# Softmax denominators of a decoder layer: partition sums by VectorE block transposes in 37 group halves, gated sums ahead in 4 instead of 19

## The chip, the cores and the metric

The kernel runs on one core of one Trainium2 chip. A core has TensorE (PE, matmuls into PSUM), VectorE (DVE), ScalarE (ACT), GpSimd (POOL) and SyncE (SP, which here only issues DMAs). The metric is the device time of one execution in microseconds, as the median of the runs. Everything is computed in float32.

## The reference

One decoder layer on x of shape (4, 1024, 512): a gated self-attention, a cross-attention to a context of shape (4, 1024, 384), and a small feed-forward network, each behind a layer norm and added to x. What matters here are the two attentions, 16 heads of 32 each:

```python
# phase 0, self-attention
attn = softmax(q @ k.T / sqrt(32))                       # over the keys
attn = attn * aperture[q] * expression[k]                # two gates per head
attn = attn / (attn.sum(keys) + 1e-8)
out  = attn @ v
# phase 1, cross-attention
out  = softmax(q @ k.T / sqrt(32)) @ v
```

With e = exp(scores), phase 0 needs two sums over the keys for every head and query: the plain one, S = sum e, and the gated one, G = sum e * expression. The output is (e * expression) @ v, divided by G + 1e-8 * S / aperture. Phase 1 needs S alone.

## The kernel before

The work is cut into eight units u: phase 0 for the batches 0 to 3 (u = 0 to 3), then phase 1 for them (u = 4 to 7). A unit has two halves hf of 512 queries each, a half has four groups g of four heads. A triple (u, hf, g) is a group half; there are 64. Each of them runs over eight key tiles kt of 128 keys, so there are 512 steps.

A step (`step`, with `scores` and `times`) does this. TensorE computes the scores of four heads (L641) with the keys on the partitions and 512 queries along the free dimension, into two PSUM tiles of two heads; ScalarE takes the exponential of each (L647) into a tile e of shape 128 x 2 x 512. The pool of e has six buffers, that is three steps. One step later TensorE multiplies e with the values (L707, into the PSUM tile av). Between steps stands other work of TensorE, spread by `run` and `beside`: the projections of the next unit, the output projection of the last (L107) and the feed-forward network. Every engine has its instructions in the order in which the program issues them; nothing is reordered at run time.

The sums over keys are sums over partitions and over key tiles. They are made in several ways:

- es[0] (heads 0 and 1): VectorE adds the eight e tiles, elementwise (L669, L671), into a 128 x 2 x 512 tile. In phase 0 it also adds e times the gate into eg (L678 on ScalarE for the first key tile, L679). In phase 1 es[1] (heads 2 and 3) is added in the same way.
- Phase 0, heads 2 and 3: TensorE sums over the partitions. For every two key tiles one round of four matmuls (L717, in `times`) with two columns, ones and the gate, accumulates into the PSUM tile sm.
- `gated` names 19 group halves in which VectorE adds the first 4 or 6 key tiles of heads 2 and 3 ahead, plain into exa (L685, L687) and gated into exb (L691 on ScalarE, L692), so that one round of L717 over exa and exb stands for the rounds of those key tiles.

When a group half ends, `normalize` (called one step late, in the step of the next group's key tile 0) copies av and sm out of PSUM (L733, L735) and leaves `add_up` for the next step, behind that step's scores. `add_up` sums es and eg (or both es) over the partitions by one more round of four matmuls with a column of ones (L746), lets ScalarE copy the result (L747), and sends it through DRAM (L752 to L762) so that the 4 x 512 sums come back as 128 x 16, in the tile c. `divide`, two steps later, computes the reciprocal on VectorE (L770 to L785) and sends it through DRAM again (L786, L790) to 128 x 512; `multiply` (L797), two steps after that, scales the unnormalised output in q. es0 and es1 have one buffer each; eg shares its buffer with es1. In the last unit most groups are summed in a mixed way (`shared`, `added_up`), and the last group half closes in a way of its own (`settle`).

Two functions put things off: `after(n, f)` runs f n steps later, at the head of that step, before its scores, or behind them where it says `behind`.

```python
c, s1, s2 = cs_[i % 2], sum1_d[i % 4], sum2_d[i % 4]
after(apart(g), lambda: divide(g, i, c))
```

All DMAs named here are issued by SP, in one queue, where an issue that waits holds back those behind it.

Of the kernel before, what the change touches and what calls it, by code (L numbers as in the profile page):

```python
# [10 lines left out]
F32 = mybir.dt.float32  # L11
U32 = mybir.dt.uint32
AF = mybir.ActivationFunctionType
ALU = mybir.AluOpType
AX = mybir.AxisListType

P = 128
B, T, D = 4, 1024, 512
H, DH = 16, 32
NPR = H // 2  # L20
HG = 4
# [4 lines left out]
HALF = 512  # L26
M, INNER = 64, 16
# [12 lines left out]
NB = 32  # L40
# [29 lines left out]
def moderate_path(tc: tile.TileContext, a: dict, out: bass.AP, flag: bass.AP):  # L70
    nc = tc.nc
    x = a["x"]
    with ExitStack() as st:
        enter = st.enter_context
        const = enter(tc.tile_pool(name="mconst", bufs=1))
        dram = enter(tc.tile_pool(name="mdram", bufs=1, space=bass.MemoryType.DRAM))
# [4 lines left out]
        p1 = enter(tc.tile_pool(name="mp1", bufs=1))  # L81
        p2 = enter(tc.tile_pool(name="mp2", bufs=2))
# [35 lines left out]
        iap_d = [[dram.tile([H, HALF], F32, tag=f"iap_{b}_{i}", name="iap_d") for i in range(2)] for b in range(B)]  # L118
        sum1_d = [dram.tile([HG, HALF], F32, tag=f"sum1_{i}", name="sum1_d") for i in range(4)]
        sum2_d = [dram.tile([2, HG, HALF], F32, tag=f"sum2_{i}", name="sum2_d") for i in range(4)]  # L120
        rec_d = [dram.tile([HG, HALF], F32, tag=f"rec_{i}", name="rec_d") for i in range(4)]
        wout_d = dram.tile([P, NC, D], F32, name="wout_d")

# [2 lines left out]
        fixed = const.tile([P, 3], F32, name="fixed")  # L126
        ones, share, power = (fixed[:, i : i + 1] for i in range(3))
        pick = const.tile([P, 3], F32, name="pick")
        nc.gpsimd.memset(pick, 0.0)
        nc.gpsimd.memset(pick[:, 1:2], 1.0)  # L130
        for one, is_ in ((ones, 1.0), (power, -0.5), (share, 1.0 / M)):
            nc.gpsimd.memset(one, is_)

        NS = 2 * B * 2 * HG
        marks = const.tile([P, 2 * NS + B * NT], F32, name="marks")
# [56 lines left out]
        cs = p1.tile([P, 2, NC], F32, name="cs")  # L192
# [107 lines left out]
        av = pa.tile([P, HALF], F32, tag="av", name="av")  # L300
        nc.vector.memset(av, 0.0)
        sm = pa.tile([P, HALF], F32, tag="sm", name="sm")
        nc.vector.memset(sm, 0.0)


        cs_ = [const.tile([P, 2, 2, INNER], F32, name=f"cs{i}") for i in range(2)]
        for t in cs_:
            nc.gpsimd.memset(t, 0.0)

        S = {}  # L310
        crossing = []
# [62 lines left out]
        def after(steps, f, behind=False):  # L374

            soon.append((tick[0] + steps, behind, f))
# [236 lines left out]
        def attention(u, hf):  # L613

            ph, b = order[u]
            me = S[u]
            steps = []
            sums = 2 if ph == 0 else 1

            def shared(g):  # L620
                return ph == 0 or (u + 1 == len(order) and not (g == 1))

            added_up = {(0, 0): (0, 4), (0, 2): (0,), (0, HG - 1): (0, 4), (1, 0): (0,), (1, 2): (0,)} if u + 1 == len(order) else {}

            gated = {(0, 1, 0): 4, (0, 1, 1): 4, (0, 1, 2): 4, (0, 1, 3): 6, (1, 0, 0): 4, (1, 1, 0): 4, (1, 1, 1): 4, (1, 1, 2): 4, (1, 1, 3): 6, (2, 0, 0): 4, (2, 1, 0): 6, (2, 1, 1): 4, (2, 1, 2): 4, (2, 1, 3): 6, (3, 0, 0): 4, (3, 0, 3): 4, (3, 1, 0): 4, (3, 1, 1): 4, (3, 1, 3): 4}

            def apart(g):
                return 2 if u + 1 < len(order) else 3
# [100 lines left out]

            def normalize(g):  # L730
                i = (u * 2 + hf) * HG + g
                both = p1.tile([P, 2, HALF], F32, tag="both", name="both")
                nc.scalar.copy(me["q", hf][:, g, :], av)  # L733
                if shared(g):
                    nc.scalar.copy(both[:, 0, :], sm)  # L735
                    added = [me["es"][0][:, 0, :], me["es"][0][:, 1, :]]
                    if ph == 0:
                        added += [me["eg"][:, 0, :], me["eg"][:, 1, :]]
                else:
                    added = [me["es"][h // 2][:, h % 2, :] for h in range(HG)]  # L740
                after(1, lambda: add_up(g, i, both, added), behind=True)

            def add_up(g, i, both, added):

                for j, e in enumerate(added):
                    nc.tensor.matmul(sm[j * DH : j * DH + 1, :], lhsT=ones, rhs=e, start=True, stop=True)  # L746
                nc.scalar.copy(both[:, 1, :], sm)  # L747

                c, s1, s2 = cs_[i % 2], sum1_d[i % 4], sum2_d[i % 4]
                rows = both.rearrange("(j r) s q -> j r s q", r=DH)  # L750
                n = len(added)
                nc.sync.dma_start(s1[0:n], rows[0:n, 0, 1, :])  # L752
                if not shared(g):
                    nc.sync.dma_start(c[:, 0, 0, :], s1[0:n].rearrange("h (q e) -> (h q) e", e=INNER))
                else:
                    for k in range(sums):
                        nc.sync.dma_start(s2[k], rows[:, k, 0, :])
                    nc.sync.dma_start(
                        c[0:64, 0:sums, 0, :], s1[0:n].rearrange("(s h) (q e) -> (h q) s e", h=2, e=INNER)
                    )  # L760
                    for k in range(sums):
                        nc.sync.dma_start(  # L762
                            c[64:, k, :, :], s2[k].rearrange("(p h) (q e) -> (h q) p e", h=2, e=INNER)
                        )
                after(apart(g), lambda: divide(g, i, c))

            def divide(g, i, c):
                if shared(g):
                    both_ = p2.tile([P, sums, INNER], F32, tag="c2", name="both_")
                    nc.vector.tensor_tensor(both_, c[:, 0:sums, 0, :], c[:, 0:sums, 1, :], ALU.add)  # L770
                else:
                    both_ = c[:, 0:1, 0, :]
                if ph == 0:

                    den = p2.tile([P, INNER], F32, tag="den", name="den")
                    nc.vector.scalar_tensor_tensor(
                        den, both_[:, 0, :], 1e-8, me["iap", hf][:, g, :], ALU.mult, ALU.mult
                    )
                    nc.vector.tensor_tensor(den, den, both_[:, 1, :], ALU.add)
                else:  # L780
                    den = both_[:, 0, :]
                rec = p2.tile([P, INNER], F32, tag="rec", name="rec")
                nc.vector.reciprocal(rec, den)
                nc.vector.tensor_reduce(marks[:, i : i + 1], den, AX.X, ALU.add)
                nc.vector.tensor_reduce(marks[:, NS + i : NS + i + 1], rec, AX.X, ALU.add)  # L785
                nc.sync.dma_start(rec_d[i % 4].rearrange("j (q e) -> (j q) e", e=INNER), rec)  # L786

                all_ = p1.tile([P, HALF], F32, tag="recb", name="recb")
                for j in range(HG):
                    nc.sync.dma_start(  # L790
                        all_[j * DH : (j + 1) * DH, :], rec_d[i % 4][j : j + 1, :].to_broadcast([DH, HALF])
                    )
                after(apart(g) + (u + 1 == len(order) and g < 2), lambda: multiply(g, all_), behind=u + 1 < n or g < HG - 1)

            def multiply(g, all_):
                own = me["q", hf][:, g, :]
                nc.vector.tensor_tensor(own, own, all_, ALU.mult)  # L797
                me["divided", hf] = g
# [22 lines left out]
        def settle(u, hf, g):  # L821

            me = S[u]
            i = (u * 2 + hf) * HG + g
            rec = p1.tile([P, HALF], F32, tag="recb", name="recb")
            den = p1.tile([P, 2, HALF], F32, tag="both", name="den")[:, 0, :]
            few = p2.tile([P, INNER], F32, tag="rec", name="few")
            column = den.rearrange("p (b j) -> p b j", j=NB)[:, :, 0]

            def sums():  # L830
                me["by ones"](me["rest"], False, False)
                me["by ones"](me["e", NT - 1], False, True)

            def divide(part):
                cols, own = ts(part, HALF // 2), ts(part, INNER // 2)
                nc.vector.transpose(den[:, cols], sm[:, cols])
                nc.vector.reciprocal(few[:, own], column[:, own])
                nc.vector.transpose(rec[:, cols], few[:, own].unsqueeze(2).to_broadcast([P, INNER // 2, NB]))
                nc.vector.tensor_tensor(me["q", hf][:, g, cols], av[:, cols], rec[:, cols], ALU.mult)

            def look():
                nc.vector.tensor_reduce(marks[:, i : i + 1], column, AX.X, ALU.add)
                nc.vector.tensor_reduce(marks[:, NS + i : NS + i + 1], few, AX.X, ALU.add)

            return sums, divide, look
# [377 lines left out]
        p = pres[0]  # L1223
# [28 lines left out]
        sums, divide, look = settle(n - 1, 1, HG - 1)  # L1252
# [8 lines left out]
        h = [part for item in held[0]["h"] for part in item]  # L1261
# [671 lines left out]
```

## Time and profile before

| | |
|---|---|
| runs, median | 2135.34 us (2134.0 to 2136.43, three runs) |
| profiled execution | 2137.01 us, of which the span is 2135.2 us |
| granted TensorE clock | 0.998 of full speed |
| L641, scores | 7992 records, 589.3 us busy |
| L707, e times values | 4096 records, 548.2 us busy |
| L717 on e and the gates | 688 records, 89.5 us busy |
| L746, sums of es and of eg | 356 and 128 records, 65.3 and 32.8 us busy |
| L679, gated additions into eg | 448, 315.2 us busy |
| L692, gated additions into exb | 130, 91.4 us busy |
| L685 and L687, additions into exa | 19 and 46, 23.1 and 55.9 us busy |

A row of the profile names the line of the kernel, the engine, the operation, the tile that is written and those that are read, how often it ran, its busy time and the mean of one. Busy times of matmuls overlap: four matmuls on 32 columns each run side by side, so a row's sum is less than count times mean. One float32 matmul appears as two records. The span is cut into 40 slices whose digits are tenths of busy time; a timeline gives start and duration of each instruction, merged where the same follows itself, with the idle time before it and what ended it in brackets.

### The profile page before, as it was taken

What the parts mean: (1) busy time and instruction counts of PE and PEld (TensorE: products, weight loads), DVE (VectorE), ACT (ScalarE), POOL (GpSimd) and SP (SyncE); (2) the same over time, 40 slices, a digit from 0 to 9 for tenths busy, and PEclk for the clock granted to TensorE, in tenths of its full rate; (3) what the DMA queues carried; (4) which work ended last, traced back from release to release, by engine and by line L of the source; (5) the groups of instructions that cost most, each with busy time, mean ns of one, the idle gap of its engine ahead of it and who ended that gap; (6) DMA issues with size and microseconds to landing.
All of it is one profiled execution on the core that took longest, in us unless ns stands there. A gap on an engine that the chain in (4) does not pass through costs nothing.

```text
span 2135.2 us, 52477 instructions
## 1 busy us (share of the span) xinstructions
PE 2118.0 (99%) x22380; PEld 551.5 (26%) x22380; DVE 1677.9 (79%) x2468; ACT 1255.8 (59%) x1537; POOL 139.3 (7%) x184
## 2 busy tenths in 40 slices
PE   9999999999999999999999999999999999999998
PEld 5322222222222222222222222222222222222223
DVE  3477789888898888977889666887788778778887
ACT  0156555655556565565766666565655656567774
POOL 2000000040030100001000010000000000000001
PEclk9999999999999999999999999999999999999999
DMA  5422234132231212212222212231432213232231
GB/s 149 118 71 54 68 82 125 25 83 78 77 109 42 86 39 71 72 43 72 67 77 72 72 52 71 83 99 51 106 86 81 81 52 71 71 91 70 73 91 50
DMA packets 154495, 161.79 MB, mean 76 GB/s; under 512 B 47366, under 2 KB 93062, under 8 KB 153100
## 3 DMA queue, kind: packets, MB, share of 16 engines
q1 hardware_dynamic: 150188, 156.26, 25.4%
q8 instruction: 177, 2.90, 0.6%
q0 software_dynamic: 2080, 0.98, 0.3%
q10 hardware_dynamic: 1984, 1.12, 0.2%
q14 instruction: 66, 0.54, 0.1%
HBM read 115.53 MB, written 42.73 MB: 74 GB/s over the span
## 4 chain that ended last, share of the span: by engine, by line
PE 55%; DVE 1%; issue 0%; ACT 0%; DVEq 0%; ACTq 0%
PE f L107 19%; PE s L641 15%; PE av L707 14%; PE sm L746 2%; PE sm L717 2%; PE f L990 1%; PE f L641 1%; PE f L1068 0%; PE s L107 0%; DVE res L1076 0%; PE f L1024 0%; DVE es L671 0%; ACT e L647 0%; PE s L1068 0%; PE sm L697 0%
## 5 line engine op out<-in xcount | busy, mean ns | idle before, releaser
L647 ACT ACTIVATE e<-s 128x1024 f32<-128x1024 f32 x999 | 971.6, 1023 | 684.9 <-PE s L641 479.6
L671 DVE TENSOR_TENSOR es<-es,e 128x1024 f32<-128x1024 f32 x541 | 649.7, 1226 | 123.2 <-ACT e L647 121.9
L641 PE MATMUL s<-q,k 32*64 32x512 f32 x7992 | 589.3, 613 | 0.5 <-ACT e L647 0.2
L707 PE MATMUL av<-e,v 128*32 128x512 f32 x4096 | 548.2, 603 | 0.0
L107 PE MATMUL f<-xT,w 128*32 128x512 f32 x2816 | 333.7, 592 | 0.7 <-DVE xT L347 0.7
L679 DVE SCALAR_TENSOR_TENSOR eg<-e,sw,eg 128x512 f32<-128x512 f32 x448 | 315.2, 744 | 9.0 <-ACT eg L678 9.0
L669 DVE TENSOR_TENSOR es<-e 128x1024 f32<-128x1024 f32 x96 | 114.7, 1221 | 188.3 <-ACT e L647 176.6
L107 PE MATMUL f<-w,q 128*32 128x512 f32 x1984 | 238.6, 592 | 0.2
L641 PEld LDWEIGHTS s<-q,k 32*64 32x64 f32 x7992 | 129.1, 129 | 415.9 <-ACT e L647 199.5
L707 PEld LDWEIGHTS av<-e,v 128*32 128x32 f32 x4096 | 87.8, 108 | 402.9 <-issue 402.5
L107 PEld LDWEIGHTS f<-xT,w 128*32 128x32 f32 x2816 | 91.8, 110 | 211.4 <-issue 205.2
L107 PE MATMUL f<-w,xT 128*32 128x512 f32 x896 | 106.0, 592 | 0.6 <-DVE q L321 0.6
L107 PEld LDWEIGHTS f<-w,q 128*32 128x32 f32 x1984 | 64.7, 110 | 150.4 <-issue 142.2
L107 PE MATMUL f<-ctxT,w 128*32 128x512 f32 x768 | 92.3, 592 | 0.0
L107 PE MATMUL f<-w,ctxT 128*32 128x512 f32 x768 | 92.3, 592 | 0.0
L692 DVE SCALAR_TENSOR_TENSOR exb<-e,sw,exb 128x512 f32<-128x512 f32 x130 | 91.4, 743 | 0.0
L899 POOL TENSOR_TENSOR r<-res,bo_bc 128x512 f32<-128x512 f32 x32 | 40.9, 1279 | 747.0 <-DVE res L891 598.9
L717 PE MATMUL sm<-e,sw 128*2 128x512 f32 x688 | 89.5, 592 | 0.0
L327 POOL TENSOR_SCALAR rs<-fmv 128x4 f32<-128x4 f32 (+2 forms) x18 | 11.9, 659 | 833.6 <-DVE fmv L896 833.3
L746 PE MATMUL sm<-es,fixed 128*1 128x512 f32 x356 | 65.3, 591 | 0.0
L687 DVE TENSOR_TENSOR exa<-exa,e 128x1024 f32<-128x1024 f32 x46 | 55.9, 1216 | 0.0
L891 DVE TENSOR_TENSOR res<-f,res 128x512 f32<-128x512 f32 x62 | 42.4, 683 | 16.6 <-PE f L107 9.6
(293 smaller groups left out, 1354.7 us busy)
## 6 DMA issues: line engine op xcount, KB each, us to landing
recb<-rec_d SPq DMA_DIRECT2D x252, 64.0 KB
xT<-rows_d SPq DMA_DIRECT2D x60, 256.0 KB
rows_d<-r SPq DMA_DIRECT2D x60, 256.0 KB
w<-in_xattn_Wo SPq DMA_DIRECT2D x9, 1024.0 KB
w<-wout_d SPq DMA_DIRECT2D x8, 1024.0 KB
res<-in_x SPq DMA_DIRECT2D x32, 256.0 KB
x1b_d<-r SPq DMA_DIRECT2D x32, 256.0 KB
res<-x1b_d SPq DMA_DIRECT2D x32, 256.0 KB
```

The source lines that it names most:

```text
L107: nc.tensor.matmul(to[r], lhsT=lhsT[:, j, :] if len(lhsT.shape) == 3 else lhsT[:, r], rhs=rhs, **flags)
L641: nc.tensor.matmul(two[j][m : m + 64], lhsT=k[r, g, kt * P + m : kt * P + m + 64], rhs=q[r, g, :], start=True, stop=True,)
L647: nc.scalar.activation(e[:, h, :] if len(reads) == 1 else e[:, h.start, :], s, AF.Exp, scale=SCALE)
L669: nc.vector.tensor_tensor(me["es"][i], me["e", begin][i], es[i], ALU.add)
L671: nc.vector.tensor_tensor(me["es"][i], me["es"][i], es[i], ALU.add)
L679: nc.vector.scalar_tensor_tensor(eg, es[0][:, h, :], gate(kt), eg, ALU.mult, ALU.add)
L687: nc.vector.tensor_tensor(me["ep"], me["ep"], es[1], ALU.add)
L692: nc.vector.scalar_tensor_tensor(et, es[1][:, h, :], gate(kt, h), et, ALU.mult, ALU.add)
L707: nc.tensor.matmul(av[r, :], lhsT=me["v"][:, kt, HG * g + h, :], rhs=es[h // 2][:, h % 2, :], start=(kt == 0), stop=(kt == NT - 1),)
L717: nc.tensor.matmul(sm[j * DH : j * DH + sums, :], lhsT=lhsT, rhs=rhs, start=start, stop=stop)
L746: nc.tensor.matmul(sm[j * DH : j * DH + 1, :], lhsT=ones, rhs=e, start=True, stop=True)
L891: nc.vector.tensor_tensor(r, res["po"], r, ALU.add)
```

## The change

In 37 group halves (`flat`: 26 of phase 0, 11 of phase 1) a new function `fold` takes the place of `add_up`. VectorE transposes each of the four 128 x 512 sums in blocks of 32 x 32, reading the elements of a block 16 apart, and reduces the transposed blocks along the free dimension. That leaves one partial sum for each quarter of the partitions. They go to DRAM (`parts_d`) and come back side by side as four columns (`four`), and `divide` adds the four. `turn(0)` runs in `normalize`, in the step of the next group's key tile 0, `turn(1)` and the DMAs at the head of the step after; `divide` stays where it was. `gated` has four entries instead of nineteen, all with 4 key tiles. The transposes write into exa's buffer in phase 0 and into that of `both` in phase 1. The two cleared tiles `cs_` become one tile `four`, whose unwritten half is no longer read. Three memsets of constants at the start stand ahead of two others.

```diff
         sum2_d = [dram.tile([2, HG, HALF], F32, tag=f"sum2_{i}", name="sum2_d") for i in range(4)]
+        parts_d = [dram.tile([P, HG, INNER], F32, tag=f"parts_{i}", name="parts_d") for i in range(4)]
         rec_d = [dram.tile([HG, HALF], F32, tag=f"rec_{i}", name="rec_d") for i in range(4)]
...
         pick = const.tile([P, 3], F32, name="pick")
+        for one, is_ in ((ones, 1.0), (power, -0.5), (share, 1.0 / M)):
+            nc.gpsimd.memset(one, is_)
         nc.gpsimd.memset(pick, 0.0)
         nc.gpsimd.memset(pick[:, 1:2], 1.0)
-        for one, is_ in ((ones, 1.0), (power, -0.5), (share, 1.0 / M)):
-            nc.gpsimd.memset(one, is_)
 
...
 
-        cs_ = [const.tile([P, 2, 2, INNER], F32, name=f"cs{i}") for i in range(2)]
-        for t in cs_:
-            nc.gpsimd.memset(t, 0.0)
 
...
 
-            gated = {(0, 1, 0): 4, (0, 1, 1): 4, (0, 1, 2): 4, (0, 1, 3): 6, (1, 0, 0): 4, (1, 1, 0): 4, (1, 1, 1): 4, (1, 1, 2): 4, (1, 1, 3): 6, (2, 0, 0): 4, (2, 1, 0): 6, (2, 1, 1): 4, (2, 1, 2): 4, (2, 1, 3): 6, (3, 0, 0): 4, (3, 0, 3): 4, (3, 1, 0): 4, (3, 1, 1): 4, (3, 1, 3): 4}
+            gated = {(0, 1, 3): 4, (1, 1, 3): 4, (2, 1, 0): 4, (2, 1, 3): 4}
+
+            flat = ((0, 0, 0), (0, 0, 1), (0, 0, 3), (0, 1, 0), (0, 1, 1), (0, 1, 2), (0, 1, 3), (1, 0, 0), (1, 0, 3), (1, 1, 0), (1, 1, 1), (1, 1, 2), (1, 1, 3), (2, 0, 0), (2, 0, 3), (2, 1, 0), (2, 1, 1), (2, 1, 2), (2, 1, 3), (3, 0, 0), (3, 0, 1), (3, 0, 2), (3, 0, 3), (3, 1, 0), (3, 1, 2), (3, 1, 3), (4, 0, 0), (4, 0, 1), (4, 0, 2), (4, 0, 3), (4, 1, 0), (5, 0, 1), (5, 0, 2), (5, 1, 0), (6, 0, 1), (6, 0, 2), (6, 1, 0))
 
...
                 i = (u * 2 + hf) * HG + g
+                nc.scalar.copy(me["q", hf][:, g, :], av)
+                if (u, hf, g) in flat:
+                    return fold(g, i)
                 both = p1.tile([P, 2, HALF], F32, tag="both", name="both")
-                nc.scalar.copy(me["q", hf][:, g, :], av)
                 if shared(g):
...
 
+            def fold(g, i):
+                tiles = [me["eg"], me["es"][0]] if ph == 0 else [me["es"][0], me["es"][1]]
+                at = (1, 0) if ph == 0 else (0, 1)
+                parts = p1.tile([P, 2, 2, INNER], F32, tag="parts", name="parts")
+                own, to = parts_d[i % 4], p1.tile([P, 2, 4, INNER], F32, tag="four", name="four")
+                if ph == 0:
+                    both = p1.tile([P, 2, HALF], F32, tag="both", name="both")[:, 0, :]
+                    nc.scalar.copy(both, sm)
+                    rows, s2 = both.rearrange("(j r) q -> j r q", r=DH), sum2_d[i % 4]
+                    for k in range(2):
+                        nc.sync.dma_start(s2[k], rows[:, k, :])
+                    for k in range(2):
+                        nc.sync.dma_start(
+                            to[64:, k, 0:2, :], s2[k].rearrange("(p h) (q e) -> (h q) p e", h=2, e=INNER)
+                        )
+
+                def turn(k):
+                    w = p1.tile([P, 2, INNER, NB], F32, tag="exa" if ph == 0 else "both", name="turned")
+                    for h in range(2):
+                        nc.vector.transpose(w[:, h], tiles[k][:, h, :].rearrange("p (i e) -> p e i", e=INNER))
+                    nc.vector.tensor_reduce(parts[:, at[k]], w, AX.X, ALU.add)
+
+                def rest():
+                    turn(1)
+                    nc.sync.dma_start(own, parts.rearrange("p k h e -> p (k h) e"))
+                    if ph == 0:
+                        for k in range(2):
+                            for h in range(2):
+                                nc.sync.dma_start(
+                                    to[h * DH : (h + 1) * DH, k],
+                                    own[:, 2 * k + h, :].rearrange("(a i) e -> i a e", i=DH),
+                                )
+                    else:
+                        for h in range(HG):
+                            nc.sync.dma_start(
+                                to[h * DH : (h + 1) * DH, 0], own[:, h, :].rearrange("(a i) e -> i a e", i=DH)
+                            )
+
+                turn(0)
+                after(1, rest)
+                after(1 + apart(g), lambda: divide(g, i, to))
+
             def add_up(g, i, both, added):
 
                 for j, e in enumerate(added):
                     nc.tensor.matmul(sm[j * DH : j * DH + 1, :], lhsT=ones, rhs=e, start=True, stop=True)
                 nc.scalar.copy(both[:, 1, :], sm)
 
-                c, s1, s2 = cs_[i % 2], sum1_d[i % 4], sum2_d[i % 4]
+                c, s1, s2 = p1.tile([P, 2, 4, INNER], F32, tag="four", name="four"), sum1_d[i % 4], sum2_d[i % 4]
                 rows = both.rearrange("(j r) s q -> j r s q", r=DH)
...
                         nc.sync.dma_start(
-                            c[64:, k, :, :], s2[k].rearrange("(p h) (q e) -> (h q) p e", h=2, e=INNER)
+                            c[64:, k, 0:2, :], s2[k].rearrange("(p h) (q e) -> (h q) p e", h=2, e=INNER)
                         )
                 after(apart(g), lambda: divide(g, i, c))
 
             def divide(g, i, c):
-                if shared(g):
+                if (u, hf, g) in flat:
                     both_ = p2.tile([P, sums, INNER], F32, tag="c2", name="both_")
-                    nc.vector.tensor_tensor(both_, c[:, 0:sums, 0, :], c[:, 0:sums, 1, :], ALU.add)
+                    r = slice(0, 64 if ph == 0 else P)
+                    nc.vector.tensor_reduce(
+                        both_[r], c[r, 0:sums].rearrange("p k a e -> p k e a"), AX.X, ALU.add
+                    )
+                    if ph == 0:
+                        nc.vector.tensor_tensor(both_[64:], c[64:, :, 0, :], c[64:, :, 1, :], ALU.add)
+                elif shared(g):
+                    both_ = p2.tile([P, sums, INNER], F32, tag="c2", name="both_")
+                    nc.vector.tensor_copy(both_[0:64], c[0:64, 0:sums, 0, :])
+                    nc.vector.tensor_tensor(both_[64:], c[64:, 0:sums, 0, :], c[64:, 0:sums, 1, :], ALU.add)
                 else:
                     both_ = c[:, 0:1, 0, :]
                 if ph == 0:
```

## The prediction

> **What bounds the kernel now.** I read the busy table and the slices first, then the TensorE timeline across one group boundary, then VectorE's timeline over the same stretch, then single rows for the operations that the change adds.
>
> The page of the kernel before, busy time and slices:
>
> ```profile
> PE 2118.0 (99%) x22380; PEld 551.5 (26%) x22380; DVE 1677.9 (79%) x2468; ACT 1255.8 (59%) x1537; POOL 139.3 (7%) x184
> PE   9999999999999999999999999999999999999998
> DVE  3477789888898888977889666887788778778887
> ```
>
> TensorE is busy in every slice; from 150 to 2100 us it is idle for 1.3 us of 1950 (stretches: 1749.05 of 1750 and 199.64 of 200). So TensorE's instruction stream is the time: a round of matmuls that goes shortens the span by its own length, and nothing else helps. VectorE has 20% over the whole, but 8 or 9 tenths in many slices: the question is whether it can take the work where it is put.
>
> TensorE's timeline around one boundary (start, duration, line; a row of L746 counts the two records of one matmul, so a round of four matmuls shows as eight):
>
> ```profile
> 613.32 1.11 PE L641 MATMUL s<-q,k 32*64 32x512 f32 x16
> 614.37 0.60 PE L746 MATMUL sm<-es,fixed 128*1 128x512 f32 x2
> 614.38 0.60 PE L746 MATMUL sm<-eg,fixed 128*1 128x512 f32 x2
> 614.79 0.60 PE L746 MATMUL sm<-es,fixed 128*1 128x512 f32 x2
> 614.81 0.60 PE L746 MATMUL sm<-eg,fixed 128*1 128x512 f32 x2
> 615.22 1.04 PE L707 MATMUL av<-e,v 128*32 128x512 f32 x8
> 616.08 1.90 PE L107 MATMUL f<-xT,w 128*32 128x512 f32 x16
> 617.91 1.11 PE L641 MATMUL s<-q,k 32*64 32x512 f32 x16
> 618.95 1.06 PE L707 MATMUL av<-e,v 128*32 128x512 f32 x8
> ...
> 622.52 1.11 PE L641 MATMUL s<-q,k 32*64 32x512 f32 x16
> 623.57 1.06 PE L707 MATMUL av<-e,v 128*32 128x512 f32 x8
> 624.45 1.90 PE L107 MATMUL f<-xT,w 128*32 128x512 f32 x16
> 626.28 1.11 PE L641 MATMUL s<-q,k 32*64 32x512 f32 x16
> ```
>
> A step goes from score block to score block. With the round of L746 and 16 projection records it lasts 617.91 - 613.32 = 4.59 us; with the same 16 and no round 626.28 - 622.52 = 3.76. The round costs 0.83 us. VectorE at that boundary:
>
> ```profile
> 609.69 1.41 DVE L679 SCALAR_TENSOR_TENSOR eg<-e,sw,eg 128x512 f32<-128x512 f32 x2
> 615.58 1.23 DVE L669 TENSOR_TENSOR es<-e 128x1024 f32<-128x1024 f32 x1 [4.49 <-ACT e L647]
> ```
>
> It ends a group's last additions at 611.1 and idles 4.49 us until the next group's second key tile has its exponentials. This hole comes back at every boundary, because key tile 0 gives VectorE nothing to add; and es and eg, which the new transposes read, are final when it begins.
>
> **The change part by part.**
>
> *Rounds removed.* 37 group halves lose `add_up`, one round each: 37 x 0.83 = 30.7 us less TensorE.
>
> *Rounds added.* In phase 0 a group half runs one round of L717 for every two key tiles, four in all. Gated to 4 it skips two and adds one over exa and exb (three); gated to 6 it skips three and adds one (two). Fifteen halves go from 4 to ungated, four from 6 to 4: each gains one round, 19 in all. L717's rounds start 0.86 us before what follows them (609.77 to 610.63 in the same timeline): 19 x 0.86 = 16.3 us more. Net -14.4 us on TensorE. Counted: 58 full rounds of L746 become 21, 105 of phase 0's rounds of L717 become 124.
>
> *VectorE, removed.* 15 x 3 + 4 x 2 = 53 additions into exa at 1.22 us (L685, L687) and twice as many into exb at 0.74 (L692): 64.5 + 78.9 = 143 us. ScalarE loses 37 copies of sm at 0.59 (L747) and 30 scalings at 0.72 (L691), 43 us.
>
> *VectorE, added.* Each of the 37 runs four block transposes of 128x512 and two reductions of 1024 elements to 32, half in the step of key tile 0, half at the head of the next. The nearest rows:
>
> ```profile
> L347 DVE STREAM_TRANSPOSE xT<-xT x60: 659/669/706, 56.8 to 1864.4; 128x512 f32<-128x512 f32 x60
> L784 DVE TENSOR_REDUCE marks<-den x32: 109/111/113, 147.4 to 1190.3; 128x1 f32<-128x16 f32 x32
> L842 DVE TENSOR_REDUCE marks<-den x1: 147/147/147, 2113.5 to 2113.5; 128x1 f32<-128x16 f32 x1
> L1280 DVE TENSOR_REDUCE least<-fine x1: 319/319/319, 2117.7 to 2117.7; 128x1 f32<-128x160 f32 x1
> ```
>
> A transpose of this size takes 0.68 us on average, but reads side by side; the new ones read elements 64 bytes apart. Only L842 reads with a stride (128 bytes): 147 ns for 16 elements against L784's 111, 2.25 ns more for each. Upper bound: 0.68 + 512 x 2.25 ns = 1.83 us. A reduction lies between the 1.22 of a 1024-element addition and 1.57 (L1280 less L784, 1.44 ns an element, by 1024, plus 0.09). So a fold is 4 x 0.68 + 2 x 1.22 = 5.2 us at least, 4 x 1.83 + 2 x 1.57 = 10.5 at most. I take 7.4 (transposes halfway at 1.25), since L347 is the same operation and size but L842 alone has the stride. `divide` gains a small reduction or copy of 0.1 to 0.2 us in 48 groups, some 9 us. In all VectorE goes to 1678 - 143 + 274 + 9 = 1818 us, 86% of a 2121 us span (82% at 5.2, 91% at 10.5).
>
> [...]
>
> *Does VectorE hold?* I cut its timeline at the 63 copies of av (L733) into windows of one group half, took VectorE's busy time in each, removed the gated additions, added a fold where the group before it is folded, and changed the window by 0.86 and 0.83 us. At 5.2 us no window is over-full. At 7.4 seven are, the worst (unit, half, group) being (2, 0, 1), (5, 0, 3) and (6, 0, 3) by about 2 us, and the lag is gone one or two windows later. What a lag may be: e has six buffers, three key tiles, so ScalarE waits for an addition only when VectorE is two whole steps late, some 7.5 us of 3.76 a step. The fold lands in a hole of 4.4 to 7 us, so at 7.4 it starts the next group 1 to 3 us late, inside that. Cost: nothing; if the hole were full, up to 7.4 us a boundary, less the 7.5 of slack.
>
> *eg's buffer.* ScalarE's first copy into eg (L678) now waits for the transposes of the old eg instead of matmuls. These stand first: at 611.1 + 3.7 = 614.8 they are done, and L678 starts at 616.35. Hidden; behind it stand the next exponentials.
>
> *DMAs.* A fold issues three more on SP than `add_up`: 111 at 0.34 to 0.63 us (L786, L758), some 55 us on a queue that mostly waits. The chain is: parts out, then four loads of 64-byte pieces, then `divide` two steps after the second turn. In phase 1 the old store started at 1482.88 and its load at 1484.56; so 1.7 to land, four issues at 0.6, 1.7 to land: 5.8 us from the turn's end to `divide`, which has two steps, 7.5 us or more. If late, VectorE waits about 1 us, and its additions behind `divide` with it; covered by the same slack. SP's queue holds the xT and res loads behind the store's wait for VectorE; the old store waited there for ScalarE just as long (577 us in total).
>
> *Rest.* A single buffer "four" instead of two: its reader is done five steps before the next write. The moved memsets: 1.4 us of TensorE's first wait names `pick`; between -0.5 and +0.5, taken as 0. Score blocks that last over 1.04 us add up to 22 us, where ScalarE empties them late; 43 us less of its work may give back up to 4, taken as 0.
>
> **Sum.** The profiled execution took 2137.0 us (span 2135.2 and 1.8 around it). 2137.0 - 30.7 + 16.3 = 2122.6. The median of the runs, 2135.3, lies 1.7 below that execution: **2121 us**, 0.7% faster.
>
> **Rivals.**
>
> *Partly covered.* Folds of 9 to 10.5 us: at 10.5 my windows over-fill in 22 places, the lag reaches 6 to 9 us in units 0, 2, 4, 5 and 6, and, since the fold stands at the front of its window, 10.5 - 4.5 = 6 us on top pass the slack. Counting lag at entry + 6 - 7.5 where positive gives some 10 to 15 us: 2130 to 2136. For it: L842. Against it: one row of 16 elements.
>
> *Slower.* The same mechanism, one price on: at 12 us a fold (transposes at 2.2) the lag passes 7.5 us in seven clusters by 28 us together, in units 4 to 6 above all: 2121 + 28 = 2149. It decides from about 11 us a fold. For it: the stride. Against it: above the bound from L842.
>
> *No change.* TensorE's stream shorter, but its place taken by ScalarE: steps with eight projection records fall from 3.73 to 2.90 us, and there ScalarE has two exponentials (1.94) and the eg copies (1.33), 3.27. If each of the 13 such steps kept its old length, 13 x 0.83 = 11 us would stay: 2132. Against it: TensorE runs ahead by one score pair and the next step has 3.76.
>
> **How the numbers follow.** No change that this measurement can tell is 0.2%, 4.3 us. Forecast, 2116 to 2127 (low: score blocks give back 4; high: six clusters lose 1 us each): 0.62. Partly covered but faster, 2127 to 2131: 0.14. Within 0.2%: 0.08, from the high end of partial cover and the third rival. Slower: 0.16, the strided price above 11 us or a late `divide` on top of it. The range reaches to 2138, which leaves out about 0.11 above and 0.04 below.
>
> **What would show it.** L746's successor with 188 records instead of 484; rounds of L717 up by 152 records; TensorE still idle below 3 us between 150 and 2100; transposes from 0.68 to 1.83 us; VectorE's hole at the boundary filled. Wrong, if ScalarE's exponentials wait for VectorE's es, or score blocks stretch by more than the 22 us.

## The result: 0.3% slower, and the profile after

The changed kernel took 2141.82 us (median of 8 runs, 2139.22 to 2145.67), the kernel before 2135.22 on the same chip (8 runs, 2134.0 to 2136.61). The ratio is 1.003, with an interval of 1.002 to 1.0041. The forecast was 2121 us.

The page of the changed kernel, busy time and slices:

```profile
PE 2110.0 (99%) x22236; PEld 543.4 (25%) x22236; DVE 1788.6 (84%) x2579; ACT 1221.1 (57%) x1470; POOL 133.2 (6%) x182
DVE  3488889788897988879889798888988799888887
```

The groups that the change touches (line, engine, operation, out<-in, shapes, count | busy us, mean ns | idle us before them):

```profile
L717 PE MATMUL sm<-e,sw 128*2 128x512 f32 x960 | 125.0, 592 | 0.0
L764 DVE STREAM_TRANSPOSE turned<-es 128x512 f32<-128x512 f32 x96 | 95.3, 1032 | 0.9
L765 DVE TENSOR_REDUCE parts<-turned 128x32 f32<-128x1024 f32 x74 | 90.3, 1220 | 2.5
L764 DVE STREAM_TRANSPOSE turned<-eg 128x512 f32<-128x512 f32 x52 | 51.4, 1027 | 0.0
L790 PE MATMUL sm<-es,fixed 128*1 128x512 f32 x164 | 26.9, 591 | 0.0
L790 PE MATMUL sm<-eg,fixed 128*1 128x512 f32 x24 | 6.2, 591 | 0.0
```

TensorE did lose the rounds that were forecast: 188 records (164 + 24, now on L790) stand in place of 484. VectorE is at 84%. By these two views the change went as planned. But TensorE's busy time fell by 8 us (2118.0 to 2110.0), not by the 14.4 of the forecast, and it is busy for 1735.9 us of the 1750 from 150 to 1900, where it was busy for 1749.05 before: 13 us of idle time have come in. The list of waits says where (engine, tile, line <- who ended the wait: us in total, times, longest):

```profile
ACT e L647 <- DVE eg L679: 19.0, 6, 6.0
DVE both__3634 L815 <- DMA four<-parts_d: 14.7, 1, 14.7
DVE both__6299 L815 <- DMA four<-parts_d: 13.3, 1, 13.3
PE s L641 <- ACT e L647: 9.0, 4, 4.4
DVE both__11276 L815 <- DMA four<-parts_d: 8.0, 1, 8.0
DVE both__8852 L815 <- DMA four<-parts_d: 8.0, 1, 8.0
...
PE f L1121 <- DVE g L1110: 4.6, 2, 2.3
```

These are two things. VectorE waits up to 14.7 us in `divide` (L815) for the loads of `four`; ScalarE then waits for VectorE, and TensorE for ScalarE. And twice TensorE waits 2.3 us for a tile g of the feed-forward network.

*The late loads.* SP's timeline at the first of them, the start of unit 1, in the kernel before (start, duration, line, out<-in, count):

```profile
359.73 0.42 SPq L410 DMA_DIRECT2D xin<-in_x  x1
...
360.75 2.12 SPq L864 DMA_DIRECT2D res<-in_x  x4
370.29 2.71 SPq L112 DMA_DIRECT2D w<-in_attn_Wv  x4
382.26 0.54 SPq L752 DMA_DIRECT2D sum_d<-both  x1
```

and in the changed one:

```profile
372.84 1.10 SPq L755 DMA_DIRECT2D sum_d<-both  x2
374.56 1.29 SPq L757 DMA_DIRECT2D four<-sum_d  x2
375.89 0.59 SPq L408 DMA_DIRECT2D xin<-in_x  x1
...
377.07 2.17 SPq L917 DMA_DIRECT2D res<-in_x  x4
379.34 5.08 SPq L112 DMA_DIRECT2D w<-in_attn_Wv  x4
386.15 0.34 SPq L769 DMA_DIRECT2D parts_d<-parts  x1
393.27 1.74 SPq L773 DMA_DIRECT2D four<-parts_d  x4
```

A unit begins with bulk loads, over 4 MB: the next x, weights, the residual. In the kernel before, they were issued from 359.7 on, while nothing ahead of them waited, and were over when the sums went out at 382.26. In the changed kernel `fold` puts the copies of sm (L755, L757) onto SP in the step of key tile 0, ahead of the bulk loads; SP waits there for ScalarE's copy until 372.8, and the bulk loads go out 16 us later. VectorE has its partial sums at 376.3, but their store stands behind the bulk loads: it is issued at 386.15, and the loads that wait for its landing start at 393.27, 7.1 us later. VectorE's timeline:

```profile
375.12 1.22 DVE L765 TENSOR_REDUCE parts<-turned 128x32 f32<-128x1024 f32 x1
...
381.70 0.23 DVE L516 TENSOR_SCALAR gi<-gi 128x128 f32<-128x128 f32 x1 [0.46 <-ACT gi L515]
396.61 0.36 DVE L815 TENSOR_REDUCE both__3634<-four 64x32 f32<-64x128 f32 x1 [14.67 <-DMA four<-parts_d]
```

`divide` is written two steps after the second turn, so VectorE meets it at 382 and stands there, with the additions of the next key tiles behind it. When the six buffers of e are full, ScalarE stops, and then TensorE:

```profile
396.19 1.09 PE L641 MATMUL s<-q,k 32*64 32x512 f32 x8
401.72 1.98 PE L641 MATMUL s<-q,k 32*64 32x512 f32 x8 [4.44 <-ACT e L647]
403.63 1.94 PE L707 MATMUL av<-e,v 128*32 128x512 f32 x8
405.34 2.75 PE L107 MATMUL f<-xT,w 128*32 128x512 f32 x16
408.02 1.11 PE L641 MATMUL s<-q,k 32*64 32x512 f32 x16
```

The step lasts 11.8 us in place of 3.76, 8.1 more. Only 4.44 of the 8.1 are the wait: after it eight score records take 1.98 us (1.09 before it) and eight of L707 1.94 (1.06 elsewhere). The windows show why (us, then busy time and count of PE, PEld, DVE, ACT and POOL, granted clock, DMA share, GB/s):

```profile
396.00:400.00 4.00, 1.28 (x12) 0.21 (x8) 3.25 (x10) 0.00 (x0) 0.00 (x0) 1.00 0.06 10
400.20:403.90 3.70, 2.18 (x12) 0.50 (x16) 3.70 (x5) 1.80 (x2) 0.00 (x0) 0.50 0.31 71
404.00:408.00 4.00, 4.00 (x24) 0.72 (x16) 4.00 (x7) 1.06 (x2) 0.00 (x0) 0.62 0.00 0
```

The granted clock fell to 0.50 during the wait, and work runs on at half rate after it, until 407.05. At the start of unit 2 the same happens: the step is 7.7 us longer, of which 3.43 are the wait.

*The feed-forward network.* In the steps after (5, 1, 0) and (6, 1, 0) the fold stands ahead of an addition to g that TensorE needs. VectorE's timeline there:

```profile
1575.99 1.99 DVE L764 STREAM_TRANSPOSE turned<-es 128x512 f32<-128x512 f32 x2
1578.01 1.22 DVE L765 TENSOR_REDUCE parts<-turned 128x32 f32<-128x1024 f32 x1
1579.14 2.35 DVE L669 TENSOR_TENSOR es<-e 128x1024 f32<-128x1024 f32 x2
1581.41 0.48 DVE L1110 SCALAR_TENSOR_TENSOR g<-ring,units,g 128x256 f32<-128x256 f32 x1
```

and TensorE's:

```profile
1581.94 1.13 PE L1121 MATMUL f<-outs,g 64*128 64x512 f32 x4 [2.31 <-DVE g L1110]
```

In the kernel before, one row of VectorE's timeline and one of TensorE's:

```profile
1576.30 0.48 DVE L1057 SCALAR_TENSOR_TENSOR g<-ring,units,g 128x256 f32<-128x256 f32 x1
1577.58 1.13 PE L1068 MATMUL f<-outs,g 64*128 64x512 f32 x4
```

That addition ended at 1576.8, ahead of the same matmul at 1577.58, which did not wait. There are no buffers between the two: the matmul reads g at once.

*The account.* Both traces are cut at the score blocks into the same 512 steps, and each step's change is compared with the rounds that it lost or gained. After against before: rounds 37 x -0.83 + 19 x 0.86 = -14.4 us. Steps longer than their rounds explain: (1,0,0) +8.1, (2,0,0) +7.7 and (3,0,0) +2.0, all late loads; after (5,1,0) +2.9 and after (6,1,0) +3.5; together +24.2. Steps shorter than their rounds explain, six at starts of units and halves where the kernel before added key tiles ahead: -3.7, of which 2.6 are score blocks of up to 2.00 us that ScalarE emptied late there, behind its scalings into exb (L691); -0.3 in small ones. The first score block 1.0 us earlier. Sum +4.8; the spans differ by 2140.2 - 2135.2 = 5.0, so 0.2 us stay unexplained.

### The profile page after: what moved, and what is told of

The parts are those of the page before. It is cut to its first block, busy times and chain, and to the rows that moved or that the text cites. A ratio compares the mean times of both kernels' runs of the same rounds, so it can differ in the third digit from the quotient of the medians.

```text
span 2140.2 us, 52266 instructions
## 1 busy us (share of the span) xinstructions
PE 2110.0 (99%) x22236; PEld 543.4 (25%) x22236; DVE 1788.6 (84%) x2579; ACT 1221.1 (57%) x1470; POOL 133.2 (6%) x182
## 4 chain that ended last, share of the span: by engine, by line
PE 93%; DMA 3%; DVE 2%; issue 1%; ACT 1%; SPq 0%; POOL 0%; DVEq 0%; ACTq 0%
PE f L107 36%; PE s L641 24%; PE av L707 22%; PE sm L717 5%; PE sm L790 1%; DMA parts_d<-parts 1%; PE s L107 1%; DMA res<-in_x 1%; PE f L1043 1%; PE f L641 1%; PE f L1121 1%; ACT e L647 0%; DMA four<-parts_d 0%; DVE turned L764 0%; DVE es L671 0%
## 5 line engine op out<-in xcount | busy, mean ns | idle before, releaser
L671 DVE TENSOR_TENSOR es<-es,e 128x1024 f32<-128x1024 f32 x541 | 648.3, 1225 | 115.3 <-ACT e L647 114.2
L707 PE MATMUL av<-e,v 128*32 128x512 f32 x4096 | 551.4, 606 | 0.0
L707 PEld LDWEIGHTS av<-e,v 128*32 128x32 f32 x4096 | 84.1, 108 | 412.3 <-issue 403.9
L717 PE MATMUL sm<-e,sw 128*2 128x512 f32 x960 | 125.0, 592 | 0.0
L764 DVE STREAM_TRANSPOSE turned<-es 128x512 f32<-128x512 f32 x96 | 95.3, 1032 | 0.9
L765 DVE TENSOR_REDUCE parts<-turned 128x32 f32<-128x1024 f32 x74 | 90.3, 1220 | 2.5
L1110 DVE SCALAR_TENSOR_TENSOR g<-ring,units,g 128x256 f32<-128x256 f32 x105 | 50.2, 478 | 2.7 <-ACT ring L1103 1.8
L764 DVE STREAM_TRANSPOSE turned<-eg 128x512 f32<-128x512 f32 x52 | 51.4, 1027 | 0.0
```

Of the source, the lines that this page charges most:

```text
L671: nc.vector.tensor_tensor(me["es"][i], me["es"][i], es[i], ALU.add)
L707: nc.tensor.matmul(av[r, :], lhsT=me["v"][:, kt, HG * g + h, :], rhs=es[h // 2][:, h % 2, :], start=(kt == 0), stop=(kt == NT - 1),)
L717: nc.tensor.matmul(sm[j * DH : j * DH + sums, :], lhsT=lhsT, rhs=rhs, start=start, stop=stop)
L764: nc.vector.transpose(w[:, h], tiles[k][:, h, :].rearrange("p (i e) -> p e i", e=INNER))
L765: nc.vector.tensor_reduce(parts[:, at[k]], w, AX.X, ALU.add)
L1110: nc.vector.scalar_tensor_tensor(res["g"], res["hid"], units[:, 2, h - 1 : h], res["g"], ALU.mult, ALU.add)
```

## The experiments

The theory, A: the order on SP at unit starts costs 18 us, the folds ahead of the feed-forward network 6. The rivals: the price of the strided transposes or of VectorE's load as a whole, B; and that the rounds are not worth 0.83 and 0.86. Ratios are to the kernel before on the same chip; the changed kernel, at 1.003, would be at 2143.4 beside the first four.

### The copies of sm behind the store of the partial sums

```diff
     nc.scalar.copy(both, sm)
-    for k in range(2):
-        nc.sync.dma_start(s2[k], rows[:, k, :])
-    for k in range(2):
-        nc.sync.dma_start(to[64:, k, 0:2, :], s2[k]...)
 ...
 def rest():
     turn(1)
     nc.sync.dma_start(own, ...)
     if ph == 0:
+        for k in range(2):
+            nc.sync.dma_start(s2[k], rows[:, k, :])
+        for k in range(2):
+            nc.sync.dma_start(to[64:, k, 0:2, :], s2[k]...)
```

> The changed kernel with one edit: in phase 0 a fold's copies of sm to DRAM and back (two stores and two loads) are issued with the other DMAs of the fold, one step later, behind the store of the partial sums, and no longer in the step of key tile 0. Theory A (order on SP): at the starts of units 1, 2 and 3 these copies stand ahead of the unit's bulk loads and wait for ScalarE, so that the loads start late and the fold's store queues behind them; divide on VectorE waits 8 to 15 us, and TensorE loses about 7.1, 6.8 and 1.1 us there. Without it: 2141.8 - 15 = 2127, and divide's waits for the partial sums at those three places fall below 2 us. Theory B (VectorE is over-full because the strided transposes cost 1.0 us instead of 0.68): the edit takes no work from VectorE, so 2142 as before, with the same waits.

Measured: 2127.17 us (2126.22 to 2128.09) against 2136.96, ratio 0.9953 [0.9936, 0.9969]. SP's timeline at the start of unit 1:

```profile
356.33 0.42 SPq L408 DMA_DIRECT2D xin<-in_x  x1
...
369.48 2.79 SPq L112 DMA_DIRECT2D w<-in_attn_Wv  x4
376.94 0.34 SPq L763 DMA_DIRECT2D parts_d<-parts  x1
...
380.53 1.96 SPq L773 DMA_DIRECT2D four<-parts_d  x4
```

The bulk loads are early again, the partial sums go out at 376.94 and not at 386.15, and the 14.7 us wait at L815 is 2.3 (13.3 and 8.0 at the starts of units 2 and 3 become 1.9 and 1.3). No step at a unit start is long any more; those after (5,1,0) and (6,1,0) still are (+3.6 and +3.5). Same folds, same transposes, same load on VectorE, 16 us less: it is the order on SP. (The step (0,0,2), key tile 6, is 1.5 us longer in this run; why stays open.)

### No fold at three unit starts

```diff
-flat = (... (0, 1, 3), ... (1, 1, 3), ... (2, 1, 3), ...)
+flat = (the same without these three)
```

> The changed kernel without the folds of the last group half of units 0, 1 and 2; these three go back to the sum by TensorE, still gated to 4 key tiles. Theory A: the three stalls at the starts of units 1, 2 and 3 go (15 us), three rounds of 0.83 us come back: 2141.8 - 15 + 2.5 = 2129. Theory B: three of 37 folds less take 20 us from VectorE's 1789, less than a tenth of what the change added; at most a tenth of the 20 us lost: 2140.

Measured: 2127.84 us (2127.74 to 2129.67), ratio 0.9958 [0.9941, 0.9974]. Without these three folds 15.6 us go, although three rounds come back (2.5 us): the same 18 us, found in another way. By itself this run would not tell the order on SP from the folds' work on VectorE, since it takes away both; the run above keeps the work and changes the order alone.

### No fold ahead of the feed-forward network

```diff
-flat = (... (5, 1, 0), ... (6, 1, 0))
+flat = (the same without these two)
```

> The changed kernel without the folds of the first group of the second half of units 5 and 6. There the fold stands on VectorE ahead of the last additions of the feed-forward network, for which TensorE's next matmuls wait. Theory A in its second part: 2.9 and 3.5 us of TensorE's waits go, two rounds come back: 2141.8 - 6.4 + 1.7 = 2137, and the stalls at the starts of units 1, 2 and 3 stay. Theory B: 2 of 37 folds, at most 1 us: 2141.

Measured: 2136.85 us (2134.95 to 2140.2, ten runs), ratio 1.0002 [0.9992, 1.0011]. The waits at L1121 for g are gone, those at unit starts stay (14.4 and 13.1 us at L815). The second cause is real and separate from the first: 6.5 us net of two rounds that come back (1.7).

### Transposes that read side by side

```diff
-nc.vector.transpose(w[:, h], tiles[k][:, h, :].rearrange("p (i e) -> p e i", e=INNER))
+nc.vector.transpose(w[:, h], tiles[k][:, h, :].rearrange("p (e i) -> p e i", e=INNER))
```

> The changed kernel whose block transposes read 32 neighbouring elements a block instead of elements 16 apart; the sums are then of the wrong queries, which no time depends on. It measures the stride's price: 0.68 us for a transpose if the stride alone makes it 1.03. Theory A: VectorE gets 37 x 1.4 = 52 us less to do, and the time stays at 2140 to 2142, because divide still waits for DMAs behind the bulk loads; only the two places of the feed-forward network gain about 1 us each. Theory B: most of the 20 us lost come back: 2122 to 2128.

Measured: 2138.3 us (2136.2 to 2140.36, ten runs), ratio 1.0006 [0.9996, 1.0015]. The transposes, and the wait in `divide`:

```profile
L764 DVE STREAM_TRANSPOSE turned<-es 128x512 f32<-128x512 f32 x96 | 62.3, 686 | 0.9
```

```profile
DVE both__3634 L815 <- DMA four<-parts_d: 14.2, 1, 14.2
```

The stride costs a third of each transpose, some 51 us of VectorE in all, and little of the time: the late loads do not care. What was won, about 5 us by the runs and 3.2 by the two profiled spans, lies mostly where TensorE waits for VectorE directly (the waits at L1121 fall from 2.3 to 0.9 us each; in the changed kernel 3.4 us at half clock follow one of them). B as the main cause falls.

### Both repairs

The diffs of the first and third experiment together.

> The changed kernel with both repairs: the copies of sm are issued behind the store of the partial sums (as in the run with that edit alone), and the two folds ahead of the feed-forward network's last additions are left to TensorE. Theory A, with the two places of loss independent: 2127.2 - 6.4 + 1.7 = 2122.5, that is 0.994 of the kernel before; TensorE idle below 2 us between 150 and 2100 us, and the sum of the rounds, -35 x 0.83 + 19 x 0.86 = -12.7 us, shows almost whole. If losses merely move on to other places: 2125 to 2127.

Measured: 2120.83 us (2119.01 to 2121.88, five runs) against 2135.89, ratio 0.993 [0.9916, 0.9943]. This beats both kernels. TensorE is idle for 0.14 us between 150 and 1900 us. Its page:

```profile
PE 2101.6 (99%) x22252; PEld 542.3 (26%) x22252; DVE 1778.1 (84%) x2565; ACT 1222.2 (58%) x1472; POOL 134.1 (6%) x182
```

The account closes: 35 x -0.83 + 19 x 0.86 = -12.7, steps -2.7, the first score block 2.5 us earlier: -17.9, and the spans differ by 17.7. With these two places mended, a VectorE that is busy for 84% no longer stops TensorE. That the time equals the forecast of 2121 is partly luck: two folds fewer than forecast (+1.7 us) and steps that are 2.7 us shorter, which the forecast had at 0, nearly cancel.

### Ungating alone

```diff
-flat = (37 group halves)
+flat = ()
```

> The second part of the change alone: key tiles added ahead in 4 group halves, and no fold at all. Theory A (TensorE's stream is the time, and the rounds cost what the prediction took): 19 rounds of 0.86 us more, 16.3 us over the kernel before, 1.0077 of it, with no stall, although VectorE loses 143 us of work. If VectorE's load had been holding TensorE anywhere, less than that.

Measured: 2145.42 us (2145.03 to 2145.6), ratio 1.0045 [1.0029, 1.006], 9.5 us: less than expected. The 19 rounds are there. But six steps that were longer than their rounds in the kernel before are not any more, -5.2 us with the small ones, and the first score block starts 2.9 us earlier than in the profiled run of before (between 99.8 and 102.7 us in the profiled runs of this study, 100.5 in a kernel that is the one before but for two stores, so this part is not put down to the edit). 16.3 - 5.2 - 2.9 = 8.2, the spans differ by 8.5. So some additions ahead had cost 5 us where they stood, and the ungating costs about 11 net by the steps.

### Folds alone

```diff
-gated = {(0, 1, 3): 4, (1, 1, 3): 4, (2, 1, 0): 4, (2, 1, 3): 4}
+gated = {the nineteen of before}
```

> The first part of the change alone: the 37 folds, and the 19 gated group halves as they were. Rounds: 37 x 0.83 = 30.7 us less than before; the five places of loss stay (20 us): 2135 - 30.7 + 20 = 2125 if VectorE still holds with 143 us more than in the changed kernel. By the windows of the prediction, at the measured 6.4 us a fold, the gated halves of units 0 to 2 would be over-full by 1 to 2 us each, four in a row: 2125 to 2133.

Measured: 2155.88 us (2154.3 to 2156.66), ratio 1.0092 [1.0076, 1.0107]: worse than the change, where it was expected to be better. VectorE in its page:

```profile
PE 2109.6 (98%) x22084; PEld 542.6 (25%) x22084; DVE 1914.2 (89%) x2738; ACT 1240.5 (58%) x1500; POOL 136.9 (6%) x182
DVE  3488999989999999999999898888988899888887
```

At 89%, nine tenths in nearly every slice of phase 0, steps are longer than their rounds explain in more than 30 places, 52 us together, and the waits now name VectorE's work for TensorE itself: transposes of xT (8.9 us), res (5.7) and v (5.7). The expectation was worked out from VectorE's busy time per group half with a slack of 7.5 us; that slack is only there for the path through e. The additions that ungating removes make the room for the folds: either half alone is slower than the kernel before (1.0045 and 1.0092). Folds alone with the two repairs were not run.

### The kernel before, with two stores early

```diff
 # normalize, after nc.scalar.copy(both[:, 0, :], sm)
+if ph == 0:
+    for k in range(2):
+        nc.sync.dma_start(sum2_d[i % 4][k], both...[:, k, 0, :])
 # add_up
-for k in range(sums):
+for k in range(sums if ph else 0):
```

> The kernel before, with TensorE's sums and all gates as they were, and one edit: the two stores of sm to DRAM are issued in the step of key tile 0, where the fold has them, and not one step later. VectorE, ScalarE and TensorE do exactly the work of before. Theory A (order on SP is enough by itself): the stores hold the bulk loads of the next unit until ScalarE has copied sm, the store of the other sums queues behind the loads, and divide waits 8 to 15 us at the starts of units 1, 2 and 3: 2135 + 10 to 15 = 2145 to 2150, 1.005 to 1.007 of before. Theory B: no work is added, 2135.

Measured: 2147.48 us (2147.08 to 2149.72), ratio 1.0057 [1.0042, 1.0073]. Nothing of the change is in it but the place of two 8 KB stores on SP, and it loses 12 us. Its waits:

```profile
DVE both__6250 L775 <- DMA cs<-sum_d: 6.9, 1, 6.9
DVE both__3605 L775 <- DMA cs<-sum_d: 6.6, 1, 6.6
```

Bulk loads from 373.6 to 381.7, the sums' store at 382.16, its load not before 388.69; steps at the starts of units 1 and 2 are 13 us longer together. The order alone is enough.

### The fold's DMAs on another queue

```diff
-nc.sync.dma_start(own, ...)
+nc.gpsimd.dma_start(own, ...)      # and the four loads of to
```

> The changed kernel with the fold's store of partial sums and its four loads issued by GpSimd, on that engine's own DMA queue; the copies of sm stay on SP, in the step of key tile 0, and still hold the bulk loads back. Asked is what made the store's landing take 7 us. If it was its place behind the bulk loads in SP's queue: divide's waits at the starts of units 1, 2 and 3 fall below 4 us and the time goes to 2127 to 2130 (the two places of the feed-forward network stay). If it was the bulk loads' share of the DMA engines, whatever the queue: the waits stay above 6 us and the time is 2137 to 2143.

Measured: 2148.66 us (2146.19 to 2150.5) against 2135.25, ratio 1.0064 [1.0047, 1.0081]: as neither side expected. GpSimd's timeline at the start of unit 1:

```profile
377.10 0.56 POOL L769 DMA_DIRECT2D parts_d<-parts  x1 [31.52 <-DVE parts L765]
383.96 2.18 POOL L773 DMA_DIRECT2D four<-parts_d  x4 [6.30 <-DMA w<-wout_d]
```

The store is issued 9 us sooner than in the changed kernel, so the place in SP's queue is a part of it. But it still takes over 6 us to land (1.8 in the median of all 37), while the 16 DMA engines are 66% busy from 377 to 380 and fully from 380 to 384: the bulk loads occupy the DMA engines themselves at that time. VectorE's waits at units 1 and 2 fall only to 10.6 and 10.7 us, and the steps lose 7.2 and 8.0. And the wait at (3,1,0), 5.9 us and free in the changed kernel, is 7.5 here and costs 5.4. Another queue is no cure here; loads that are early are, as the first experiment shows.

## Why the prediction was wrong, by its own steps

**Rounds removed and added: right.** 188 records of L790, 992 - 840 = 152 more of L717, and -14.4 us; with both repairs the same prices close the account to 0.2 us.

**The fold's price: right, below the value taken.** Transposes at 1.03 us (between 0.68 and 1.83), reductions at 1.22, the low end: 4 x 1.03 + 2 x 1.22 = 6.6 us, 7.4 taken. VectorE came to 1788.6 us, 1818 forecast. Elements 16 apart made a transpose take 1.03 us in place of the 0.686 of the fourth experiment, half as much again; a reduction was not slower than an addition: 1.22 us for 1024 elements, as much as L671.

**The DMAs: wrong, and this is the step that decided.** It said: "If late, VectorE waits about 1 us, and its additions behind `divide` with it; covered by the same slack." VectorE waits 14.7, 13.3, 8.0, 8.0 and 5.9 us. The step's durations came from one place in phase 1, 1.7 us to land where the DMA engines were 4% busy (1482.8 to 1486 us in the kernel before); at a unit start, with over 4 MB under way, landing took 7.1. And it asked what stands behind the new waits on SP ("SP's queue holds the xT and res loads behind the store's wait for VectorE") for the store alone: the sm copies, moved a step ahead and so past the bulk loads, were not placed on that queue at all. The slack itself was about right: waits of 8.0 us cost 0 and 2.0, the two above 13 cost 8.

**"Does VectorE hold?": wrong in "Cost: nothing" at two places.** The slack of e's buffers was applied to all of VectorE's work, but g goes to TensorE without it: +6.4 us in the account (8.2 by the third experiment with its two rounds counted; its runs spread by 5). With VectorE fuller, the folds alone show the same for xT, res and v.

**Left out: the clock.** A stall was priced by its length; each of the two long ones cost some 4 us more (8.1 and 7.7 against waits of 4.4 and 3.4), most of it in work at half clock (some 5.3 and 6.7 us of work, half of which is lost).

**Score blocks: taken as 0, up to -4 allowed; measured -2.6**, by less work of ScalarE as that step had it.

**The rivals.** The slower one was the fold's price above 11 us; that is excluded at 6.6. Slower came by what its paragraph on the chances names in half a sentence, "a late `divide` on top of it", without a price of its own. ScalarE taking TensorE's place did not come about: steps with eight projection records and no round last 2.90 us.

## What to carry to other kernels

When an issue that waits is moved forward in a queue, list what it is moved past: a small store that waits for an engine must stand behind the bulk loads that wait for nothing, or it delays them, here by 16 us, into the moment when its own data has to travel. A slack belongs to one path: before costing added work on an engine at nothing, look for every consumer that reads from it without a buffer between. And read landing times at the place where the transfer will be, not where the DMA engines are idle: here 7.1 us against 1.7.

## What the runs showed of the hardware

In the changed kernel the granted clock of TensorE fell to 0.50 at idle times of 4.44 and 3.43 us, for 6.8 us each time. Idle times of 2.3 us at L1121 were followed by 0.50 in three cases out of four (two each in the changed kernel and in the first experiment). What followed two equal waits of 2.31 us in the changed kernel, up to 1581.94 and up to 1826.02 (windows, columns as above):

```profile
1582.00:1586.00 4.00, 4.00 (x32) 1.22 (x32) 3.73 (x6) 1.84 (x2) 0.00 (x0) 1.00 0.18 46
```

```profile
1827.00:1829.00 2.00, 2.00 (x18) 0.33 (x16) 2.00 (x4) 0.00 (x0) 0.00 (x0) 0.50 0.09 12
```

In the first experiment both waits of 2.30 us were followed by 0.50, for 3.4 us each. In the eighth the clock fell after two waits of 1.73 and 1.37 us one after the other (0.81 in the mean from 398 to 404 us, 0.86 from 404 to 408). In the changed kernel the clock changes at 400.23, 407.05, 680.12, 686.95, 1827.00 and 1830.41 us, and all these times lie whole multiples of 3.413 us apart (from the first on 2, 82, 84, 418 and 419). If this spacing is carried on as a grid, one of its lines cuts the wait that left the clock at 1.00 (the line lies at 1581.24, the idle time runs from 1579.63 to 1581.94), and the other wait of 2.31 us lies whole between two lines (1823.59 and 1827.00). That is one wait of each kind: whether the place on the grid decides, and how much idle time is enough, these runs do not show.

The landing of a 32 KB store depended here on what else was under way more than on its queue: 1.8 us in the median on GpSimd's queue and 6.1 at most, beside 4 MB of loads (ninth experiment); 7.1 behind such loads on SP's (changed kernel).
